# Layer 0 of a four-layer network: two forms of the votes in one tile, a share in a single bank, and a reciprocal moved off VectorE

## The chip, the core and the metric

The kernel runs on one core of a Trainium2 chip. Its engines are TensorE (matrix products, written to PSUM), VectorE, ScalarE, GpSimd (which does not touch PSUM here) and SyncE, whose queue issues most DMAs. The metric is device microseconds of one execution. The profile's short names are PE, PEld (TensorE's weight loads), DVE (VectorE), ACT (ScalarE), POOL (GpSimd) and SP (SyncE).

## The reference, cut to what matters

The input x is 8 images of 16 channels of 256 x 256, fp32. Four layers follow, each as x = x + layer(groupnorm(x)). The change is in layer 0 alone, a convolution whose result is routed between the eight images (axis a):

```
def squash(t, axis=0):
    norm = jnp.linalg.norm(t, axis=axis)
    n2 = norm * norm
    return n2 * t / ((1.0 + n2) * norm)
votes = conv(tensor, w)                  # 3x3, 16 -> 8*16 channels, reshaped n, atoms, cout, h, w
logits = zeros
for _ in range(3):
    r = softmax(logits, axis=0)
    preds = einsum('abcde,abde->bcde', votes, r)
    preds = squash(preds, axis=0)
    logits = logits + einsum('abcde,bcde->abde', votes, preds)
```

In the reference's letters the softmax runs over axis a, the images, the sum with weights r also over a, and the norm of the squash over b, the atoms; this is done three times for every pixel.

## The kernel before, in words

Before layer 0 the statistics of the first norm are taken (`stats0`, to about 95 us), and layers 1 to 3 come after it; none of that is changed. Layer 0 works on 64 tiles of four image rows. For each tile:

- `prepare` (L464) loads x for the tile two further on (`xs`, L470), normalizes it with one product per half (`pd`, L479) and a ScalarE move (L482) and writes it, padded, to a DRAM tensor `d0` (L491), so that rows of all channels and images lie side by side.
- The tile has two halves h of two rows each. For each h, two DMAs (L513) load `kt[h]`: 128 partitions, which are two column shifts times four padded rows times 16 channels, of all eight images. `votes` (L524) makes, for each row j and each half g of the images, one group: two whole products (128 rows of contraction, L533) for column taps 0 and 1, and two products of 64 rows (L537) for column tap 2. The four padded rows serve both j with weights that are zero where a row does not belong. ScalarE copies the group to `v[h]` (L542).
- `squash` (L561) takes a norm: two squares on ScalarE (L569), products that add over the atoms into `n2` (L573), a root by Ln and Exp on ScalarE (L587 to L589), a numerator, a denominator and a reciprocal on VectorE (L593 to L595), and one product on GpSimd (L599): the factors f, 128 x 128. This is done three times per tile.
- `factor` (L606) spreads f over the atoms by products (`fb`, L617). `logits` (L628) multiplies the prediction by it (L635), then all votes by that (`pr`, L643), and sums over c with products (`pl`, L653). In the first routing step the result goes to `ls` by a ScalarE copy (L686); in the second it is copied (L675) and added on GpSimd (L680).
- `softmax` (L691) transposes (`lg`, L700), subtracts the greatest (L706, L707), takes exp on ScalarE (L712), divides (L716 to L718), transposes back (`rt`, L724) and copies to `rs` (L733).
- `weighted` (L736) spreads `rs` by 32-row products (`rb`, L751), in terms of images (4, 5), (6), and (0, 1), (2, 3); VectorE makes `dd` from it and the votes (L762), and GpSimd adds all (L771) to `s`.
- At the end the prediction is scaled (L813), GpSimd adds x (`res`, L816), ScalarE takes statistics (L828), and SP stores the result (L839, L840, L846, L848).

Buffers are counted. `xs` and `res` share the one place of kind `io`. `kt` has two places, `v` six (three tiles in flight), `f` two, `dd` four. In PSUM, kind `x` has three places of two banks (pd, cv, fb and rb take them) and `u` two of one bank (n2, pl, lg, rt).

The order of the work is not that of the code. Each step is recorded as an operation of one engine with what it reads and writes (`_Order.op`, L226). `_Order.run` (L252) then issues, of all operations that are ready and whose buffers are free, the one with the least due time. The due time is the tile's number times a period plus an entry of the list `TIMES`, one for each operation of a tile (L256), so the list decides which tiles' work stands next to which on each engine. Engines then run their own instructions in that order and wait for each other by semaphores.

Of the kernel before, what the change touches and what calls it, by code (L numbers as in the profile page):

```python
# [10 lines left out]
F32 = mybir.dt.float32  # L11
AF = mybir.ActivationFunctionType
ALU = mybir.AluOpType
# [5 lines left out]
P = 128  # L19
WP = W + 2  # L20
# [10 lines left out]
def _consts():  # L31

    p = np.arange(P)
    hi, lo = p // 16, p % 16

    fold = np.stack([h * 16 + lo[:, None] == np.arange(32)[None, :] for h in range(2)], 1)
    unfold = np.zeros((4, 2, C, 2, 4, P), np.float32)
    for h in range(2):
        for k in range(4):
            unfold[k, h, :, h, k] = 0.5 * (np.arange(C)[:, None] == lo[None, :])  # L40


    sel = np.stack([16 * g + 8 * h + hi[:, None] == np.arange(32)[None, :] for g in range(2) for h in range(2)], 1)
    spread = np.zeros((4, 2, 2, 8, 2, 2, 8, C), np.float32)
    for g in range(2):
        for h in range(2):
            for b in range(8):
                spread[:, g, h, b, g, h, b] = 1.0

    diff = np.zeros((B, C, C, B), np.float32)  # L50
    for i in range(C):
        for a in range(B - 1):
            diff[a, i, i, a] = 1.0
            diff[B - 1, i, i, a] = -1.0
        diff[:, i, i, B - 1] = 1.0 / B
    parts = {

        "pair": 0.5 * (p[:, None] // 2 == p[None, :] // 2),
        "diff": diff.reshape(P, P),

        "fold": fold.reshape(P, 2 * 32),
        "unfold": unfold.reshape(P, 8 * P),

        "sel": sel.reshape(P, 4 * 32),

        "spread": spread.reshape(P, 4 * P),
        "ident": np.eye(P),

        "group": (lo[:, None] // 2 == lo[None, :] // 2) / 16.0,

        "same_lo": lo[:, None] == lo[None, :],
        "ones": np.ones((P, P)),
        "mean": np.full((P, P), 1.0 / P),

        "same_c4": lo[:, None] == p[None, :] % 64 // 4,

        "hi8": hi[:, None] == np.arange(8)[None, :],
        "row0": p[:, None] == np.arange(16)[None, :],

        "middle": -(p[:, None] % 4 - 1.5),  # L80

        "pad": _padding(),


        "keep": np.stack([p >= 16, (p < 48) | (p >= 64), p >= 64, p < 64], 1),

        "ident3": _ident3(),
    }
    at = 0
    cols = []  # L90
    for name, a in parts.items():
        a = np.asarray(a, np.float32)
        _CONST[name] = (at, a.shape[1])
        at += a.shape[1]
        cols.append(a)
    return np.ascontiguousarray(np.concatenate(cols, 1))
# [39 lines left out]
def _layout(w0, bw, sw, sc, bias, wq, bq, wk, bk, wv, bv, w3):  # L136
# [1 line left out]


    w0 = w0.reshape(3, 3, C, P)  # L140
    l0 = np.zeros((2, 2, 4, C, 2, P), np.float32)
    for j in range(2):
        for kh in range(3):
            for dx in range(2):
                l0[0, dx, j + kh, :, j] = w0[kh, dx]
                l0[1, dx, j + kh, :, j] = w0[kh, 2]
    l0 = l0.reshape(2, P, 2 * P).transpose(1, 0, 2)


    sw = sw.transpose(1, 4, 2, 3, 0).reshape(C, 2, 4, 81 * C).transpose(0, 2, 1, 3).reshape(64, 2 * 81 * C)  # L150
# [28 lines left out]
class _Buf:  # L179
# [10 lines left out]


TIMES = [
    -723.29, -126.96, -1287.20, -291.27, -719.97, -693.08, -625.75, -683.80, -169.92, -158.78, -153.36,
    -1032.45, -146.30, -286.26, -145.45, -1375.99, -151.90, -338.16, -261.20, -230.76, -136.99, -214.63,
    -126.67, -136.17, -143.63, -139.13, -140.10, -174.81, -899.84, -137.38, -135.05, -211.64, -133.88, -127.93,
    -109.08, -115.69, -139.61, -115.29, -118.15, -149.20, -107.32, -110.73, -165.19, -382.13, -97.75, -92.86,
    -92.25, -91.12, -89.08, -198.43, -88.34, -238.75, -240.66, -85.79, -84.47, -254.75, -133.10, -336.72,
    -223.36, -77.68, -126.26, -82.81, -264.25, -217.14, -78.43, -75.92, -107.53, -72.84, -47.31, -266.51,
    -185.51, -154.67, -555.69, -72.72, -216.04, -93.74, -182.88, -41.32, -30.68, -276.56, -149.62, -123.61,
    -28.12, -118.42, -27.48, -29.71, -88.26, -84.70, -24.63, -62.07, -138.31, -998.81, -338.10, -23.75, -71.35,  # L200
    -168.85, -21.77, -17.87, -1189.68, -15.52, -17.81, -78.48, -11.77, 13.13, -11.07, 16.57, -105.36, -162.33,
    31.16, -216.22, 15.81, 16.90, 16.88, -188.95, 24.25, 29.14, 26.46, 33.82, -255.28, -124.68, -124.23,
    -285.23, -135.30, -169.10, -92.14, -167.00, 36.88, -40.85, -558.24, -220.65, -113.85, -402.73, -159.96,
    35.14, -89.25, 53.60, 71.24, -670.06
]


# [79 lines left out]
class _Net:  # L287
# [123 lines left out]
    def layer0(self, wd, bd, less0, tiles=range(TILES)):  # L411
# [8 lines left out]
        with ExitStack() as st:  # L420
# [1 line left out]
            self.constants(one, "fold", "ident")  # L422
            sbuf = st.enter_context(tc.tile_pool(name="l0_sb", bufs=2))
            psum = st.enter_context(tc.tile_pool(name="l0_ps", bufs=1, space=PSUM))
            w = one.tile([P, 2, 2, P], F32, name="w0")
            nc.sync.dma_start(out=w.rearrange("p s j m -> p (s j m)"), in_=self.d["l0"].rearrange("p s f -> p (s f)"))
            tiny = one.tile([P, 1], F32, name="tiny")
            nc.vector.memset(tiny, 1e-18)
            stats = self.const.tile([P, 2, 2 * TILES], F32, name="st1")
            ident = self.k["ident"]  # L430
            fold = self.k["fold"].rearrange("p (h m) -> p h m", h=2)
            unfold = self.k["unfold"].rearrange("p (h k m) -> p h k m", h=2, k=4)
            sel = self.k["sel"].rearrange("p (g h m) -> p g h m", g=2, h=2)
            spread = self.k["spread"].rearrange("p (g h m) -> p g h m", g=2, h=2)
            ROW = P * WP
# [16 lines left out]
                )  # L452
            nc.sync.dma_start(out=self.d0[(H + 2) * ROW :].unsqueeze(0), in_=ring[0][0:1, 0, 0:16])

            places = dict(io=1, kt=2, v=6, sq=2, f=2, ls=3, e=2, rs=2, s=3, pr=2, dd=4)
            banks = dict(x=3, u=2)
            order = _Order({**places, **banks}, 61.05, TIMES)

            def buf(kind, shape, name=None):
                pool = psum if kind in banks else sbuf  # L460
# [36 lines left out]
            def work(i):  # L497
# [3 lines left out]
                def op(*a, **k):  # L501
                    ops.append(order.op(*a, **k))
# [1 line left out]
                if i + 2 < TILES:  # L504
                    prepare(i + 2, op)

                kt = [buf("kt", [P, 8 * WP]) for _ in range(2)]
                for h in range(2):
                    for dx in range(2):

                        def fetch(h=h, dx=dx):
                            at = (4 * i + 2 * h) * ROW + dx
                            nc.sync.dma_start(  # L513
                                out=kt[h]()[dx * 64 : dx * 64 + 64],
                                in_=self.d0[at : at + 4 * ROW].rearrange("(p f) -> p f", f=8 * WP),
                            )

                        op("SP", 0.5, fetch, [("d0", i), ("d0", i + 2 * h - 1)], [(kt[h], dx)], lag=6.0)
                res = buf("io", [P, 2, 512], "res")


                v = [buf("v", [P, 8, 512]) for _ in range(2)]

                def votes(h, j, g):  # L524


                    ps = buf("x", [P, 2, 512], "cv")

                    def products():
                        t = kt[h]().rearrange("p (a w) -> p a w", a=8)  # L530
                        for n in range(2):
                            a = 4 * g + 2 * n
                            nc.tensor.matmul(ps()[:, n], w[:, 0, j, :], t[:, a : a + 2, 0:W], start=True, stop=False)  # L533
                        for n in range(2):
                            a = 4 * g + 2 * n
                            at = slice(n * 64, n * 64 + 64)
                            nc.tensor.matmul(  # L537
                                ps()[:, n], w[at, 1, j, :], t[at, a : a + 2, 2 - n : 2 - n + W], start=False, stop=True
                            )

                    def move():
# [2 lines left out]
                            ps().rearrange("p n (a w) -> p (n a) w", w=W),  # L544
                        )

                    op("PE", 3.2, products, [(kt[h], 0), (kt[h], 1)], [(ps, 0), (v[h], "turn")], mode="votes")
                    op("ACT", 1.1, move, [(ps, 0)], [(v[h], g, j)])

                def voted(h, a):  # L550
                    return [(v[h], a // 4, 0), (v[h], a // 4, 1)]

                for g in (1, 0):
                    for h in range(2):
                        for j in range(2):
                            votes(h, j, g)

                def rows(ap):
                    return ap.rearrange("p (r w) -> p r w", w=W)
# [1 line left out]
                def squash(s, read):  # L561
# [29 lines left out]
                    def divide():  # L591
                        t, u, den, q = (f()[:, n] for n in range(4))
                        nc.vector.scalar_tensor_tensor(den, n2(), 1.0, t, ALU.add, ALU.mult)  # L593
                        nc.vector.tensor_tensor(u, u, n2(), ALU.add)
                        nc.vector.reciprocal(den, den)  # L595

                    def times():
                        t, u, den, q = (f()[:, n] for n in range(4))
                        nc.gpsimd.tensor_tensor(q, u, den, ALU.mult)  # L599

                    op("ACT", 1.1, root, [(n2, 0)], [(f, 2)])
                    op("DVE", 1.3, divide, [(n2, 0), (f, 2)], [(f, 4)])
                    op("POOL", 0.4, times, [(f, 4)], [(f, 3)])
                    return f

                def factor(f, h, also=()):  # L606
# [4 lines left out]
                    def products():  # L611
                        for b in also:
                            b()
                        for n in range(2):
                            for j in range(2):
                                at = slice(64 * j, 64 * j + 64)
                                nc.tensor.matmul(  # L617
                                    fb()[:, j, n * P : n * P + P],
                                    unfold[at, h, 2 * j + n, :],
                                    f()[at, 3],  # L620
                                    start=True,
                                    stop=True,
# [113 lines left out]
                def weighted(rs):  # L736
# [3 lines left out]
                    for h in range(2):  # L740

                        def term(images, h=h):

                            rb = [buf("x", [P, 2, 512], "rb") for _ in images]

                            def products():
                                for pair, r in zip(images, rb):
# [982 lines left out]
```

## Time and profile before

| | us |
|---|---|
| median of the runs shown (three) | 6453.93 |
| lowest and highest | 6452.06, 6459.32 |
| the profiled execution | 6451.19 |
| its span | 6448.7 |
| layer 0, steady part | from about 200 to about 3330 |

The profiled execution's granted clock was 0.989. In the page, each digit of the slices is the busy share of a fortieth of the span (161 us) in tenths. A group's row names line, engine, operation, written and read tiles, shapes and count, then busy time and the mean of one, and last the idle time before it on its engine with what ended it. A TensorE product of fp32 shows as two instructions, so "x4" is two products. Busy times of matmuls overlap, so blocks are better read in the timeline, from the start of one to the start of the next. The chain of waits follows the work that ended last back through whatever released each step.

### The profile page before, as it was taken

Reading aid. Unit: us, or ns where it says so; the run is one execution under the profiler, and the core shown is the slowest. Engines: PE = TensorE matmul, PEld = TensorE weight load, DVE = VectorE, ACT = ScalarE, POOL = GpSimd, SP = SyncE. Lnnn points to the kernel's source line nnn. Section 1 sums busy time; section 2 is a strip of 40 time slices with the busy share of each in tenths; the row PEclk is TensorE's granted clock in tenths of the full one; section 3 lists DMA queues with packets and bytes.
Section 4 is the critical chain, followed back from the end, with each engine's and each line's share of the span. In section 5 each row is a group of like instructions: output and inputs, shape, how many; then the busy total and the mean of one; then the engine's idle time right before and its main releaser. Section 6 shows DMA issues by size and latency. Waiting matters only on the chain.

```text
span 6448.7 us, 109346 instructions
## 1 busy us (share of the span) xinstructions
PE 6078.3 (94%) x44488; PEld 2716.0 (42%) x44488; DVE 5060.9 (78%) x5963; ACT 2967.9 (46%) x4474; POOL 3394.3 (53%) x2464
## 2 busy tenths in 40 slices
PE   2999999999999999999995999999999999999998
PEld 1333333333333333333332444444444566666653
DVE  5788888888888888888886999999999633333331
ACT  0344444444444444444433888888888422112221
POOL 0577777777777777777775434334433211111123
PEclk9999999999999999999996999999999999999999
DMA  7333333333333333333323555555556543434358
GB/s 270 77 94 99 98 98 92 92 98 93 100 96 100 92 92 98 92 101 94 100 69 95 184 180 173 175 178 174 176 180 179 158 82 90 89 83 93 90 176 267
DMA packets 379593, 800.62 MB, mean 124 GB/s; under 512 B 57426, under 2 KB 191154, under 8 KB 343890
## 3 DMA queue, kind: packets, MB, share of 16 engines
q1 hardware_dynamic: 335250, 730.35, 40.4%
q0 software_dynamic: 9856, 29.20, 1.6%
q10 hardware_dynamic: 33984, 34.08, 1.5%
q8 instruction: 349, 5.72, 0.4%
q14 instruction: 154, 1.26, 0.1%
HBM read 582.77 MB, written 210.77 MB: 123 GB/s over the span
## 4 chain that ended last, share of the span: by engine, by line
PE 58%; DVE 32%; issue 4%; DMA 3%; ACT 1%; POOL 1%; SPq 0%; DVEq 0%; POOLq 0%; ACTq 0%
PE cv L533 13%; PE cv L537 7%; PE pqk L1455 7%; DVE bases L1009 7%; PE pl L653 6%; PE rb L751 5%; DVE e L999 4%; DVE pr L643 4%; PE po L1482 4%; DVE dd L762 4%; PE psc L1470 3%; PE pv L1462 3%; PE p L1547 3%; DVE a L999 2%; DVE a L978 2%
## 5 line engine op out<-in xcount | busy, mean ns | idle before, releaser
L771 POOL TENSOR_TENSOR dd<-dd 128x1024 f32<-128x1024 f32 x512 | 1209.0, 2361 | 338.7 <-DVE dd L762 318.4
L1032 PE MATMUL ps<-bases,tw 128*32 128x512 f32 (+1 forms) x13824 | 1361.7, 545 | 16.7 <-POOL bases L1001 6.7
L762 DVE SCALAR_TENSOR_TENSOR dd<-rb,v 128x1024 f32<-128x1024 f32 (+1 forms) x1024 | 1078.0, 1084 | 214.3 <-PE rb L751 175.5
L1001 POOL TENSOR_TENSOR bases<-e,a 128x1024 f32<-128x1024 f32 (+1 forms) x264 | 621.7, 2378 | 928.1 <-DVE e L999 927.8
L542 ACT COPY v<-cv 128x1024 f32<-128x1024 f32 x512 | 518.7, 1013 | 1281.2 <-PE cv L537 1281.2
L643 DVE TENSOR_TENSOR pr<-v,fb 128x2048 f32<-128x2048 f32 (+1 forms) x512 | 1010.9, 2015 | 32.0 <-PE pl L653 28.1
L533 PE MATMUL cv<-kt,w 128*128 128x512 f32 x2048 | 1009.1, 615 | 11.2 <-DMA kt<-d 9.4
L1032 PEld LDWEIGHTS ps<-bases,tw 128*32 128x32 f32 x13824 | 598.2, 109 | 801.7 <-issue 482.9
L771 POOL TENSOR_TENSOR s<-s,dd 128x512 f32<-128x512 f32 x512 | 653.3, 1276 | 30.1
L751 PE MATMUL rb<-rs,ct_fold 32*128 32x512 f32 x3584 | 605.6, 649 | 9.1 <-ACT rs L733 2.4
L533 PEld LDWEIGHTS cv<-kt,w 128*128 128x128 f32 x2048 | 347.0, 189 | 558.8 <-issue 392.7
L537 PE MATMUL cv<-kt,w 64*128 64x512 f32 x2048 | 578.8, 641 | 0.0
L653 PE MATMUL pl<-pr,ct_fold 128*32 128x512 f32 x3584 | 531.6, 605 | 45.4 <-DVE pr L643 45.2
L1466 ACT ACTIVATE vt<-pv,w_b2v 128x128 f32<-128x128 f32 x512 | 146.5, 368 | 840.2 <-PE pv L1462 840.2
L771 POOL TENSOR_TENSOR s<-v,dd 128x512 f32<-128x512 f32 x256 | 325.9, 1273 | 340.0 <-DVE dd L762 330.9
L1455 PE MATMUL pqk<-w_qk,t 128*128 128x512 f32 x1024 | 482.9, 594 | 4.7 <-POOL t L1449 4.6
L1487 DVE TENSOR_TENSOR y<-po,res 128x512 f32<-128x512 f32 x128 | 88.5, 691 | 493.9 <-PE po L1482 468.5
L1009 DVE SCALAR_TENSOR_TENSOR bases<-xr,xm,bases 128x1024 f32<-128x1024 f32 (+1 forms) x264 | 447.9, 1734 | 0.3 <-POOL bases L1001 0.3
L1449 POOL TENSOR_TENSOR t<-t,emb 128x512 f32<-128x512 f32 x128 | 162.5, 1270 | 514.0 <-DVE t L1445 494.3
L986 ACT ACTIVATE sq<-a 128x1024 f32<-128x1024 f32 (+1 forms) x264 | 263.7, 999 | 231.4 <-DVE a L978 230.7
L968 ACT ACTIVATE d<-xr,bd,sd 128x1024 f32<-128x1024 f32 (+1 forms) x264 | 319.0, 1208 | 14.1 <-DMA xr<-x1p 14.1
L751 PEld LDWEIGHTS rb<-rs,ct_fold 32*128 32x128 f32 x3584 | 173.0, 185 | 351.0 <-issue 118.2
(269 smaller groups left out, 8430.3 us busy)
## 6 DMA issues: line engine op xcount, KB each, us to landing
kt<-d SPq DMA_DIRECT2D x256, 516.0 KB
xr<-x1p SPq DMA_DIRECT2D x120, 1024.0 KB
d<-dn ACTq DMA_DIRECT2D x64, 516.0 KB
x<-y SPq DMA_DIRECT2D x128, 258.0 KB
xs<-in_x_dram SPq DMA_DIRECT2D x16, 2048.0 KB
xs<-in_x_dram SPq DMA_DIRECT2D x64, 512.0 KB
res<-in_x_dram SPq DMA_DIRECT2D x64, 512.0 KB
x<-s SPq DMA_DIRECT2D x128, 256.0 KB
```

Source lines behind the costliest of these rows:

```text
L533: nc.tensor.matmul(ps()[:, n], w[:, 0, j, :], t[:, a : a + 2, 0:W], start=True, stop=False)
L537: nc.tensor.matmul(ps()[:, n], w[at, 1, j, :], t[at, a : a + 2, 2 - n : 2 - n + W], start=False, stop=True)
L542: nc.scalar.copy(v[h]()[:, 4 * g : 4 * g + 4, j * W : j * W + W], ps().rearrange("p n (a w) -> p (n a) w", w=W),)
L643: nc.vector.tensor_tensor(pr()[:, :n].rearrange("p n (r w) -> p n r w", w=W), v[h]()[:, 4 * g : 4 * g + n].rearrange("p n (r w) -> p n r w ...
L653: nc.tensor.matmul(pl()[at : at + 32], sel[:, g, h, :], pr()[:, t, :], start=h == 0 and g == 0, stop=h == 1 and (g == 1 or t == 3),)
L751: nc.tensor.matmul(r()[:, n], spread[at, g, h, :], rs()[at], start=True, stop=True)
L762: nc.vector.scalar_tensor_tensor(dd()[:, :n], r()[:, :n], 1.0 / B, v[h]()[:, a : a + n], ALU.subtract, ALU.mult)
L771: op("POOL", us, lambda: nc.gpsimd.tensor_tensor(out[0](), a[0](), b[0](), ALU.add), a[1] + b[1], out[1])
L1001: nc.gpsimd.tensor_tensor(ring[n % 3][:, 0, p : p + m, 1 : 1 + W], rows(e), rows(a), ALU.subtract)
L1009: nc.vector.scalar_tensor_tensor(r, rows(part[1]), xm[:, b : b + 1], v, ALU.is_gt, ALU.mult)
L1032: nc.tensor.matmul(out if k is None else out[:, k], lhs, rhs, start=start, stop=stop, skip_group_check=True)
L1455: nc.tensor.matmul(ps, t[:, n, k * P : (k + 1) * P], wqk[:, n, :], start=n == 0, stop=n == 1)
```

## The change

Four things are changed, all in layer 0.

1. Votes in two forms. For h = 1 nothing but names changes (`wide`, `votes_wide`). For h = 0 each row j gets loads of its own: `kt` holds eight of the nine taps times 16 channels in 128 partitions (two DMAs), and `kr` holds the ninth, in four groups of 32 partitions, one for each pair of images (one DMA; the upper 16 partitions of a group have the tap's weights, the others zeros). Then `rest` makes four products of 32 rows into two `x` buffers, and `most` adds two whole products to each. The weights `l0` now hold both forms, 768 columns in place of 512.
2. The lone share of a term, image 6, takes a one-bank buffer of kind `u` (`r6`) instead of a two-bank one of kind `x`.
3. The reciprocal in the squash: instead of VectorE's, ScalarE takes Ln and Exp with scale -1, and GpSimd does one Newton step, four operations instead of one.
4. `TIMES` is a new list, with an entry for each operation of the new tile, and the period in the due times is 48 instead of 61.05.

The constant `unfold` also becomes half as wide, since both pairs of its blocks were alike.

```
-            order = _Order({**places, **banks}, 61.05, TIMES)
+            places = dict(io=1, kt=2, kr=2, v=6, sq=2, f=2, ls=3, e=2, rs=2, s=3, pr=2, dd=4)
+            order = _Order({**places, **banks}, 48, TIMES)
...
+                def votes(h, j):
+                    kt = buf("kt", [P, 8 * WP])
+                    kr = buf("kr", [P, 2 * WP])
+                    at = (4 * i + 2 * h + j) * ROW
...
+                    def fetch():
+                        rows_at(kt()[:96], 0, [[1, 2], [8 * WP, 48], [1, 8 * WP]])
+                    def fetch2():
+                        rows_at(kt()[96:], 2, [[8 * WP, 32], [1, 8 * WP]])
+                    def fetch3():
+                        rows_at(kr(), 16 * 8 * WP + 2, [[2 * WP, 4], [8 * WP, 32], [1, 2 * WP]])
...
+                    ps = [buf("x", [P, 2, 512], "cv") for _ in range(2)]
+                    def most(g):
+                        t = kt().rearrange("p (a w) -> p a w", a=8)
+                        for n in range(2):
+                            a = 4 * g + 2 * n
+                            nc.tensor.matmul(ps[g]()[:, n], w[:, 0], t[:, a : a + 2, 0:W], start=False, stop=True)
+                    def rest():
+                        for g in range(2):
+                            for n in range(2):
+                                at = slice(64 * g + 32 * n, 64 * g + 32 * n + 32)
+                                t = kr()[at].rearrange("p (a w) -> p a w", a=2)[:, :, 0:W]
+                                nc.tensor.matmul(ps[g]()[:, n], w[at, 1], t, start=True, stop=False)
+                    op("PE", 1.1, rest, [(kr, 0)], [(p, 0) for p in ps] + [(v[h], "turn")], mode="last")
...
-                for g in (1, 0):
-                    for h in range(2):
+                for h in range(2):
+                    if h in (0,):
                         for j in range(2):
-                            votes(h, j, g)
+                            votes(h, j)
+                    else:
+                        wide(h)
...
-                        nc.vector.reciprocal(den, den)
+                    def inverse():
+                        t, den = f()[:, 0], f()[:, 2]
+                        nc.scalar.activation(t, den, AF.Ln)
+                        nc.scalar.activation(t, t, AF.Exp, scale=-1.0)
                     def times():
-                        t, u, den, q = (f()[:, n] for n in range(4))
-                        nc.gpsimd.tensor_tensor(q, u, den, ALU.mult)
+                        r, u, den, q = (f()[:, n] for n in range(4))
+                        nc.gpsimd.tensor_tensor(den, den, r, ALU.mult)
+                        nc.gpsimd.tensor_tensor(q, u, r, ALU.mult)
+                        nc.gpsimd.tensor_scalar(den, den, -1.0, 2.0, ALU.mult, ALU.add)
+                        nc.gpsimd.tensor_tensor(q, q, den, ALU.mult)
...
-                            rb = [buf("x", [P, 2, 512], "rb") for _ in images]
+                            rb = [buf("x", [P, 2, 512], "rb") if len(a) == 2 else buf("u", [P, 1, 512], "r6") for a in images]
```

## The prediction

> **What bounds the kernel now.** First the page's busy row and slices, then a table of windows, to see where layer 0 lies and which engine fills it:
>
> ```profile
> PE 6078.3 (94%) x44488; PEld 2716.0 (42%) x44488; DVE 5060.9 (78%) x5963; ACT 2967.9 (46%) x4474; POOL 3394.3 (53%) x2464
> ...
> PE   2999999999999999999995999999999999999998
> ...
> POOL 0577777777777777777775434334433211111123
> ```
>
> ```profile
> 1200.00:1600.00 400.00, 383.19 (x2264) 144.95 (x2266) 358.64 (x381) 170.86 (x298) 306.05 (x203) 1.00 0.37 97
> 1600.00:2000.00 400.00, 383.20 (x2284) 144.99 (x2280) 357.42 (x384) 169.38 (x298) 303.33 (x204) 1.00 0.37 97
> ```
>
> The columns are TensorE, its weight loads, VectorE, ScalarE, GpSimd, the granted clock, the DMA share and GB/s. Layer 0 is steady from about 200 to 3330 us, at full clock. One tile of four rows takes 51.36 us: in the chain of the window 800 to 2800 the same VectorE piece stands at 838.85 and, 38 tiles on, at 2790.37. Of these 51.36, TensorE is busy 49.2, VectorE 46.0, GpSimd 38.9, ScalarE 21.8.
>
> Next the groups of the window 800 to 2800, forms kept apart (busy, mean ns):
>
> ```profile
> L533 PE MATMUL cv<-kt,w 128*128 128x512 f32 x1248 | 613.8, 614 | 0.4
> L751 PE MATMUL rb<-rs,ct_fold 32*128 32x512 f32 x2180 | 359.7, 640 | 4.0
> L537 PE MATMUL cv<-kt,w 64*128 64x512 f32 x1248 | 352.2, 641 | 0.0
> L595 DVE RECIPROCAL f<-f 128x128 f32<-128x128 f32 x117 | 110.4, 944 | 0.0
> L599 POOL TENSOR_TENSOR f<-f 128x128 f32<-128x128 f32 x116 | 53.1, 457 | 9.8 <-DVE f L595 9.8
> ```
>
> Mean matmul times hold the pipeline, so I price blocks by the timeline of one tile, from start to next start:
>
> ```profile
> 1658.81 1.14 PE L751 MATMUL rb<-rs,ct_fold 32*128 32x512 f32 x8
> 1659.88 1.99 PE L533 MATMUL cv<-kt,w 128*128 128x512 f32 x4
> 1661.80 1.13 PE L537 MATMUL cv<-kt,w 64*128 64x512 f32 x4
> 1662.86 1.14 PE L751 MATMUL rb<-rs,ct_fold 32*128 32x512 f32 x6
> 1664.73 0.66 PE L724 MATMUL rt<-ct_fold,e 128*128 128x128 f32 x4 [0.74 <-DVE e L718]
> ```
>
> A block of four 32-row products (eight instructions) takes 1.07, two whole products (x4) 1.92, the 64-row block 1.06 (0.96 ahead of fb). A vote group is 2.88 to 2.98, on average 2.95. A tile holds eight vote groups (23.6), eight rb blocks (8.55), four sevens of pl (7.7), six fb (3.25), three n2 (1.65), two lg and two rt (2.25) and pd (1.85): 48.85. The other 2.5 are waits: 0.74 for the softmax above, about 0.55 each at pd (VectorE's dd) and pl (VectorE's pr), the rest in small ones.
>
> Last, the chain between 1100 and 1220. In some tiles it leaves TensorE and runs through the load of x:
>
> ```profile
> 1145.48 2.51 POOL s L816 x2
> ...
> 1150.28 1.32 SPq L846
> 1151.64 7.80 DMA xs<-in_x_dram
> 1159.58 1.96 PE pd L479 x4
> ```
>
> xs and res share one buffer, so xs can be asked for only after GpSimd's last add, and in the queue it stands behind five stores. Alone, at the start (chain at 104.76), the load took 3.65. So TensorE bounds layer 0, with VectorE 5.4 us behind.
>
> **Votes, h = 0 only.** Removed per tile: four vote groups, 4 x 2.95 = 11.8. Added, for each of two j: one block of four 32-row products (L751's row, 1.07) and four whole products (2 x 1.92 = 3.84), together 2 x 4.91 = 9.82. TensorE falls by 1.98 to 46.87. The 32-row block is the same form as L751, on four row groups and four banks; bounds are 1.07 and, did the four not overlap, 3.84 as for whole products. I take 1.07, since rows and shape are those of the row. The rows hold the change of row grouping: 1.06 instead of 0.96 where the next block has another grouping.
>
> By the Trainium skill, "TensorEngine Tiling (Array Packing)", Key Properties, changing the tiling mode drains TensorE, which speaks against mixed forms. Read by the rows that drain is about 0.1 per change and the new form has no more changes, so the sum would be unmoved; were a drain worth a whole 32-row block, four of them would undo the gain. No row here shows such a drain.
>
> Moves to v stay at eight ScalarE copies of 1.01. What moves is the loads: h = 0 now loads two kt and two kr, 2.6 MB instead of 1.03, so a tile moves about 6.5 MB instead of 4.9 (96 GB/s x 51.36), and the DMA share goes from 0.37 to about 0.5. SP issues eight loads for four. Two kt places serve three loads: the wide load can start only when the first kt of the tile has been read, and it is used after rb, rb, pl, fb, lg, the next 32-row block, four whole products and rt: 1.07 + 1.07 + 1.92 + 0.54 + 0.54 + 1.07 + 3.84 + 0.59 = 10.6. The first kt load (chain at 113.27) took 8.32, so it is hidden. If it took 12, it would cost 1.4 a tile, 90 us.
>
> **Reciprocal.** VectorE loses 3 x 0.944 = 2.83 a tile: 43.1. ScalarE gains six operations like L588 (0.31): 23.7 with ample idle time. GpSimd gains nine small ones: 9 x 0.457 = 4.1, so 43.0. Its tensor_scalar is in no row; bounds are the 128x2 copy (0.19) and the 128x512 add (1.27); I take L599's 0.457, the same size. None of this is TensorE's time; what counts is whether f is late for fb. The chain from n2 was root 1.05, VectorE 1.34, GpSimd 0.46 and four hops of 0.1: 3.25. Now it is 1.05 + 0.45 + 0.65 + 1.83 and five hops: 4.5. TensorE's work between n2 and fb was 4.9, 5.3 and 11.2; in the new order it is 7.9 (four whole products, two rb, pl), 6.5 (half a pl, fb, a vote group, rb, half a pl) and 7.0 (pl, fb, rb, lg, a vote group). The cover left is 3.4, 2.0 and 2.5, for queueing; before it was 1.65, 2.05 and 7.9. Where it is gone, each microsecond of lateness is one of TensorE's, 64 us over the tiles. Behind the new wait on ScalarE stand the pl copy and the softmax's exp; behind that on GpSimd the next dd adds.
>
> By the Trainium skill, "GPSIMD Engine Reference", 4.1 Engine selection, elementwise work belongs on VectorE, since GpSimd takes about twice as long for two inputs. The trace agrees: 457 ns (L599) against 276 (L594) for the same tile. By engine time alone the edit is a loss of about 1.05 us a squash, 200 us in all if it lay on the path; by the idle 12 us that GpSimd has in each tile it is nothing.
>
> **Single-bank share.** The lone rb product goes to pool u (r6), so a term takes one two-bank buffer of three instead of two. In the new order each r6 follows a u buffer that was read before. Between no gain and the 0.5 at pd, I count it within the waits below.
>
> **Order.** I laid one period of the new order out by these durations. Four waits of TensorE remain: the second half of a 32-row block and the fb after it, whose x buffers VectorE's dd frees late (0.4 + 0.3); rb behind a vote copy (0.1); lg right behind pl with only fb (0.54) beside ScalarE's copy, 0.6 plus hops (0.3); the other lg, behind GpSimd's ls add, which stands after a 2.36 and two 1.27 adds (0.8). Sum 1.9, against 2.5 before; period 46.87 + 1.9 = 48.8. The load of xs now stands ahead of the stores: some 6.4 us of cover against 3.65 alone, so that loop no longer ends last (7.80 would cost 1.4).
>
> **Sum.** 64 x (51.36 - 48.8) = 164 us. Filling is the same chain of loads; draining, the last tile's three squashes have no cover, 3 x 1.25 = 4. The profiled execution took 6451.2 (span 6448.7): 6451.2 - 164 + 4 = 6291. The median of the runs shown is 2.7 above it: **6294 us**.
>
> **Rivals.**
> 1. The gain is half given back: f or ls on GpSimd, now 43 of 49 us busy and in order, comes late behind 2.36 us adds. For: two of the three covers are under 2.6, little over one add. Against: three tiles are in flight. Waits of 3.2 give 50.1 and 6453.9 - 81 + 4 = 6377.
> 2. Slower: the same queue, but each f starts a 2.36 and a 1.27 add later than laid out. Then 3.63 less the covers is 0.2 + 1.6 + 1.1 = 2.9 more waiting, 4.8 in all, period 51.7: 6453.9 + 22 + 4 = 6480. It decides from 4.5 us of waits a tile. For it: GpSimd shows waits of up to 4.9 us for dd, so its work is bunched. Against: before, f waited 9.8 us in 39 tiles. TensorE would pay more if a wait passed some 3 us: after 4.0 idle at 3390.43 pl x8 took 1.93 instead of 1.06.
> 3. Nothing comes of it: the loop through xs, or a kt load, still sets 51.3. About 6455. Against: the stores are moved behind xs.
>
> **How the numbers follow.** Forecast 0.69, rival 1 0.17, rival 2 0.10, rival 3 0.04. About 0.2% is what a measurement can tell from no change: faster 0.86, same 0.04, slower 0.10. Low end: half the waits (0.9), 47.8, 6453.9 - 228 + 4 = 6230. High end: waits of 4.0, 50.85, 6453.9 - 33 + 4 = 6425, past rival 1; out are rivals 2 and 3 and a small tail.
>
> **What would show it.** Right: a period near 48.8, vote lines 2 us less per tile, no reciprocal of f on VectorE, GpSimd near 43 of 49, r6 without waits. Wrong: TensorE waiting for f or ls on GpSimd by more than 1 us a time, waiting for kt or xs, a 32-row vote block over 1.2, or GpSimd's small operations over 0.6.

## The result

The changed kernel takes 7036.45 us (median of four, 7024.81 to 7041.18) beside 6455.55 for the kernel before on the same chip: a ratio of 1.0897, 95% interval 1.0878 to 1.0916. The forecast was 6294. The profiled execution took 7024.81, its span is 7023.0.

**The profile after.** The page's busy row, two of its slices, the chain, and the two whole-product vote groups:

```profile
PE 6156.0 (88%) x44488; PEld 2783.7 (40%) x44488; DVE 4918.4 (70%) x5771; ACT 3074.2 (44%) x4858; POOL 3607.6 (51%) x3040
...
PE   1788888888888888888888779999999999999998
...
PEclk8999999999999999999999889999999999999999
...
DMA d<-dn 14%; DMA kt<-d 11%; PE cv L586 8%; PE pqk L1534 6%; DVE bases L1088 6%; PE cv L590 4%; DVE e L1078 4%; PE po L1561 3%; PE psc L1549 3%; PE pv L1541 3%; PE rb L830 3%; PE p L1626 3%; DVE a L1078 2%; DVE a L1057 2%; DVE e L1057 2%
```

```profile
L586 PE MATMUL cv<-kt,w 128*128 128x512 f32 x1024 | 602.2, 718 | 359.5 <-DMA kt<-d 358.2
...
L549 PE MATMUL cv<-kt,w 128*128 128x512 f32 x1024 | 573.1, 712 | 217.7 <-DMA kt<-d 217.7
```

TensorE no longer fills layer 0, and it waits for loads of `kt`: 358 us at the wide votes (L586), 218 at the new ones (L549). No engine's own work heads the chain any more, but two DMAs: the write of `d0` and the load of `kt`. Between 800 and 2800 us a tile takes 59.83 (the residual add's semaphore at 817.4 and, 33 tiles on, at 2791.9) in place of 51.36. The first residual add is at 342.6 in place of 272.2, so the start is 70 us later too: the first load of `kt` stands in the chain with 39.63 us, where it took 8.32 before.

One tile. First TensorE's timeline, then the chain of the same stretch (start, us, what):

```profile
2046.42 1.14 PE L556 MATMUL cv<-kr,w 32*128 32x512 f32 x8
2050.95 5.29 PE L549 MATMUL cv<-kt,w 128*128 128x512 f32 x8 [3.38 <-DMA kt<-d]
2056.07 0.60 PE L803 MATMUL rt<-ct_fold,e 128*128 128x128 f32 x4
2062.72 3.75 PE L586 MATMUL cv<-kt,w 128*128 128x512 f32 x4 [6.05 <-DMA kt<-d]
2066.40 1.83 PE L590 MATMUL cv<-kt,w 64*128 64x512 f32 x4
```

```profile
2032.67 16.42 DMA d<-dn
2049.14 0.57 SPq L528
2050.37 12.22 DMA kt<-d
2062.72 3.75 PE cv L586 x4
```

And the DMA engines in the same stretch (last two columns: DMA share, GB/s; the one before is the granted clock):

```profile
2034.00:2036.00 2.00, 2.00 (x18) 0.45 (x11) 2.00 (x2) 1.97 (x6) 2.00 (x3) 1.00 1.01 303
...
2038.00:2040.00 2.00, 2.00 (x6) 0.83 (x5) 2.00 (x4) 1.09 (x3) 1.92 (x2) 1.00 0.13 56
...
2046.00:2048.00 2.00, 1.57 (x12) 0.57 (x11) 1.70 (x3) 0.00 (x0) 1.67 (x2) 1.00 0.13 56
2048.00:2050.00 2.00, 0.00 (x0) 0.00 (x0) 1.27 (x3) 0.58 (x1) 1.92 (x2) 1.00 0.12 50
...
2052.00:2054.00 2.00, 2.00 (x4) 0.94 (x3) 2.00 (x2) 0.00 (x0) 1.78 (x2) 0.50 1.02 187
```

From 2038 to 2050 the share is 0.12 to 0.13, two of sixteen DMA engines, at 50 to 56 GB/s, while TensorE first works and then stands still. The packets in it are the new `kt` load's, 8256 bytes, 0.313 us each, and packets of the `d0` write, 1032 bytes, on the same two engines in turn: 46 of each between 2039 and 2047. The trace's landing events show the same by shares. Of the 16 shares of the `d0` write, 14 have landed by 2037.98, the last two at 2048.65 and 2049.09; the new load, asked for at 2028.51, has two shares in all, at 2049.60 and 2050.02. So the write of `d0` ends after 16.42 us, and SP, which works in order, holds what is behind it:

```profile
SPq L528 <- DMA d<-dn: 581.8, 33, 18.6
```

That is 17.6 us a tile at the head of SP's queue (a `kr` load), with the wide `kt` load (L609) behind it. When that load is issued, its 12.22 us are half in the open (TensorE waits 6.05). After each wait TensorE runs at half clock for some us (0.50 in the window from 2052): L549's block takes 5.29, L586's 3.75, L590's 1.83.

### The profile page after: what moved, and what is told of

The parts are those of the page before. It is cut to its first block, busy times and chain, and to the rows that moved or that the text cites. A ratio compares the mean times of both kernels' runs of the same rounds, so it can differ in the third digit from the quotient of the medians.

```text
span 7023.0 us, 110704 instructions
## 1 busy us (share of the span) xinstructions
PE 6156.0 (88%) x44488; PEld 2783.7 (40%) x44488; DVE 4918.4 (70%) x5771; ACT 3074.2 (44%) x4858; POOL 3607.6 (51%) x3040
## 2 busy tenths in 40 slices
DMA packets 404947, 902.04 MB, mean 128 GB/s; under 512 B 58194, under 2 KB 191922, under 8 KB 361042
## 4 chain that ended last, share of the span: by engine, by line
PE 40%; DMA 28%; DVE 20%; issue 5%; POOL 4%; ACT 2%; SPq 1%; DVEq 0%; POOLq 0%; ACTq 0%
DMA d<-dn 14%; DMA kt<-d 11%; PE cv L586 8%; PE pqk L1534 6%; DVE bases L1088 6%; PE cv L590 4%; DVE e L1078 4%; PE po L1561 3%; PE psc L1549 3%; PE pv L1541 3%; PE rb L830 3%; PE p L1626 3%; DVE a L1078 2%; DVE a L1057 2%; DVE e L1057 2%
## 5 line engine op out<-in xcount | busy, mean ns | idle before, releaser
L841 DVE SCALAR_TENSOR_TENSOR dd<-rb,v 128x1024 f32<-128x1024 f32 x768 | 907.9, 1217 | 27.9 <-PE r L830 12.8
L586 PE MATMUL cv<-kt,w 128*128 128x512 f32 x1024 | 602.2, 718 | 359.5 <-DMA kt<-d 358.2
L549 PE MATMUL cv<-kt,w 128*128 128x512 f32 x1024 | 573.1, 712 | 217.7 <-DMA kt<-d 217.7
L841 DVE SCALAR_TENSOR_TENSOR dd<-r,v 128x512 f32<-128x512 f32 x256 | 176.3, 689 | 829.5 <-PE r L830 821.0
L732 PE MATMUL pl<-pr,ct_fold 128*32 128x512 f32 x3584 | 505.3, 601 | 4.8 <-DVE pr L722 4.7
L549 PEld LDWEIGHTS cv<-kt,w 128*128 128x128 f32 x1024 | 220.1, 226 | 529.5 <-issue 307.0
L586 PEld LDWEIGHTS cv<-kt,w 128*128 128x128 f32 x1024 | 201.9, 219 | 546.0 <-issue 528.0
```

What stands on the lines that cost most here:

```text
L549: nc.tensor.matmul(ps[g]()[:, n], w[:, 0], t[:, a : a + 2, 0:W], start=False, stop=True)
L586: nc.tensor.matmul(ps()[:, n], w2[:, 0, j, :], t[:, a : a + 2, 0:W], start=True, stop=False)
L732: nc.tensor.matmul(pl()[at : at + 32], sel[:, g, h, :], pr()[:, t, :], start=h == 0 and g == 0, stop=h == 1 and (g == 1 or t == 3),)
L841: nc.vector.scalar_tensor_tensor(dd()[:, :n], r()[:, :n], 1.0 / B, v[h]()[:, a : a + n], ALU.subtract, ALU.mult)
```

## The experiments

**Theory A.** The new load of 96 partitions takes the two column shifts as its outermost dimension, `[[1, 2], [8 * WP, 48], [1, 8 * WP]]`. A load with an outermost count of 2 runs on 2 of the 16 DMA engines: 96 x 8256 bytes at 54 GB/s are some 15 us, and the `d0` write, which has shares on those two engines, ends late with it. **Theory B**: the number of bytes is too much (2.6 MB of `kt` and `kr` for 1.03), however the loads are cut. **Theory C**: the new order of SP's queue holds the wide load back, whatever the first load takes. **Theory D**: the reciprocal's longer chain, or the vote form, slows the kernel by itself. (The expectations number the first three in the same way.)

**1. The same load as two.**

```
-  rows_at(kt()[:96], 0, [[1, 2], [8 * WP, 48], [1, 8 * WP]])
+  for dx in range(2):
+      rows_at(kt()[48 * dx : 48 * dx + 48], dx, [[8 * WP, 48], [1, 8 * WP]])
```

> The changed kernel, but the 96-partition load of kt is made as two loads of 48 partitions, one for each column shift; bytes, buffers and order stay. Theory A (the load whose outermost dimension counts 2 runs on 2 of the 16 DMA engines: 8256-byte packets of 0.313 us, 12 to 13 in 2 us, 54 GB/s, for 14 us, and the write of d0 ends behind it): the load spreads, the write of d0 lands in under 8 us, TensorE no longer waits for kt, a tile takes 48.5 to 49.5 us, the whole 6280 to 6350. Theory B (the 1.6 MB more per tile is too much for the loads, however they are cut): over 6900, as the changed kernel's 7036. Theory C (the new order of SP's queue holds the wide load back, whatever the first load takes): over 6800.

Measured: 6306.23, ratio 0.9771 (0.9756 to 0.9785), inside theory A's range.

**2. The same single load, with the rows outermost** (the weight rows are put in the new order of partitions):

```
-  rows_at(kt()[:96], 0, [[1, 2], [8 * WP, 48], [1, 8 * WP]])
+  rows_at(kt()[:96], 0, [[8 * WP, 48], [1, 2], [1, 8 * WP]])
```

> The changed kernel with the same single load of 96 partitions and the same bytes, but its dimensions swapped: 48 rows outermost, the two shifts inside (the weights' rows are permuted to match). Theory A, if the outermost count decides how a load is spread: within 0.5% of the split kernel, 6280 to 6350. If instead only contiguous runs or the number of loads matters (A wrong in that point): still 7036. Theories B and C: about 7036.

Measured: 6274.02, ratio 0.9726 (0.9711 to 0.9740), 6 us under the expectation and 0.5% below the split load. Bytes, loads and their order in SP's queue are those of the changed kernel, and 762 us are gone. That is theory A; B and C fall, and D cannot be what made the kernel slow, since the reciprocal and the vote form are still there. The pages' packet counts fit as well: under 512 bytes there are 58194 in the changed kernel, 59986 here and 62034 with the split load, so 14 and 30 more for each of the 128 loads, as one small packet for each engine that takes part would give for 16 and twice 16 engines in place of 2. The `kr` load still has an outermost count of 4; no wait for it shows among TensorE's. The waits of TensorE, and the chain of one tile:

```profile
PE cv L587 <- DMA kt<-d: 16.5, 19, 1.9
PE lg L780 <- POOL ls L760: 13.6, 42, 0.3
PE rb L831 <- DVE pr L723: 9.0, 41, 0.2
PE cv L587 <- ACT rs L813: 5.9, 5, 1.2
PE cv L587 <- ACT v L572: 1.4, 2, 0.7
```

```profile
2041.34 7.72 DMA d<-dn
...
2050.35 10.21 DMA kt<-d
```

The `d0` write takes 7.72 for 16.42. The waits sum to 46.4 in 42 tiles, 1.1 a tile, and a tile takes 47.99 (825.4 to 2792.9, 41 tiles). The wide load still takes 10.2, the cover that the prediction laid out being 10.6, so it still ends last in 19 tiles, by 0.9 us on average.

**3. The kernel before, with this form alone**: each half's two loads of 64 partitions become one of 128 with the shift outermost. Same bytes, half the loads.

```
-  out=kt[h]()[dx * 64 : dx * 64 + 64],
-  in_=self.d0[at : at + 4 * ROW].rearrange("(p f) -> p f", f=8 * WP),
+  out=kt[h](),
+  in_=bass.AP(tensor=src.tensor, offset=src.offset, ap=[[1, 2], [8 * WP, 64], [1, 8 * WP]]),
```

> The kernel before, with nothing of the change, but the two loads of each kt (64 partitions each) are made as one load of 128 partitions with the two shifts outermost: the suspected cost alone, with the same bytes and one load fewer. Theory A: 1.03 MB on 2 engines at 54 GB/s is 19 us a load, 38 us a tile on the same two engines, the write of d0 ends behind them and TensorE waits for kt: 6700 to 7600, and a rate near 54 GB/s between bursts. Theories B and C: 6455, within 0.5%, since neither bytes nor order change.

Measured: 6892.30, ratio 1.0678 (1.0662 to 1.0694). The form costs 438 us with none of the change around it. The expectation had the size but not the place: what waits is not the product that reads `kt` but `pd`, whose load of x has shares on the same two engines. Of the one asked for at 1653.17, 14 shares have landed by 1657.46 and the last two at 1662.19 and 1662.26. In the window 800 to 2800:

```profile
PE pd L479 <- DMA xs<-in_x_dram: 179.3, 33, 7.4
```

**4. An outermost count of 3**: three shifts of two kernel rows in the 96 partitions, the other two taps in the 32 (weight rows put in that order).

```
-  rows_at(kt()[:96], 0, [[1, 2], [8 * WP, 48], [1, 8 * WP]])
+  rows_at(kt()[:96], 0, [[1, 3], [8 * WP, 32], [1, 8 * WP]])
-  rows_at(kt()[96:], 2, [[8 * WP, 32], [1, 8 * WP]])
+  rows_at(kt()[96:], 32 * 8 * WP, [[8 * WP, 16], [1, 2], [1, 8 * WP]])
```

> The changed kernel with the 96-partition load cut so that its outermost dimension counts 3 (three shifts, 32 rows each) instead of 2; the 32-partition load takes the remaining two taps with 16 outermost; same bytes, number of loads and order. Theory A in numbers: 3 engines at 26 GB/s each is 79 GB/s, the load takes about 9.8 us instead of 14.3, and stretches with 18 to 20 packets of 8256 bytes in 2 us take the place of those with 12 to 13. The tile lies between the 60.5 us of the changed kernel and the 48.7 of the spread load: 50 to 57, the whole 6380 to 6800. If it were only a matter of two against many (a special case of two), it would be about 6274; if the form of the load didn't matter, 7036.

Measured: 6942.19, ratio 1.0760 (1.0739 to 1.0782). The rate comes near the expected one; the time lies far above the expected range:

```profile
2052.00:2054.00 2.00, 2.00 (x19) 0.85 (x16) 1.37 (x2) 1.36 (x4) 2.00 (x2) 1.00 0.70 219
2054.00:2056.00 2.00, 2.00 (x23) 1.05 (x20) 1.72 (x2) 0.99 (x3) 1.92 (x2) 1.00 0.17 68
...
2060.00:2062.00 2.00, 2.00 (x22) 0.41 (x14) 2.00 (x3) 0.00 (x0) 1.92 (x5) 1.00 0.19 76
```

```profile
2049.96 15.17 DMA d<-dn
...
2066.44 10.41 DMA kt<-d
```

The share is 0.17 to 0.19, three of sixteen. By its landing events the load, asked for at 2045.80, now has three shares and ends at 2062.84: 17.0 us after issue, where the one on two engines needed 21.5 (2028.51 to 2050.02). It is not the expected 9.8, since until 2054 its engines also serve spread transfers (170 to 290 GB/s in all): my expectation took the load as alone on its engines, and that was wrong. The load became 4.5 us shorter, but the `d0` write only 1.25 (15.17 for 16.42): its small packets still take turns with the load's large ones, one for one (49 of each between 2055 and 2061), and now on three engines. So TensorE's wait for the new load is all but gone (9.0 us in the window 800 to 2800, 0.3 a tile, for 2.8), while that for the wide load, behind the write in SP's queue, is 8.5 a tile (290.0 in 34) for 5.8. The special case of two falls, and so does the sum by the load's rate alone.

The Trainium skill, "DMA: Bandwidth & Descriptors", section "Why a DMA increments its semaphore by 16 and not by 1", has the rule: the slowest dimension of each side that is not of size one is taken, and the largest number up to 16 that divides both is the number of DMA engines. For 96 partitions against 2, 3 and 48 rows this gives 2, 3 and 16. The runs agree: shares of 0.12 to 0.13 and 0.17 to 0.19 with two and three landing events, and in experiment 2 sixteen landing events and no stretch of several us near 0.12 in the tile shown.

**5. The kernel before, with the reciprocal moved alone** (ScalarE's Ln and Exp, GpSimd's Newton step; the due times of before, the new step taking that of the division):

```
-                        nc.vector.reciprocal(den, den)
+                        nc.scalar.activation(t, den, AF.Ln)
+                        nc.scalar.activation(t, t, AF.Exp, scale=-1.0)
...
-                        nc.gpsimd.tensor_tensor(q, u, den, ALU.mult)
+                        nc.gpsimd.tensor_tensor(den, den, r, ALU.mult)
+                        nc.gpsimd.tensor_tensor(q, u, r, ALU.mult)
+                        nc.gpsimd.tensor_scalar(den, den, -1.0, 2.0, ALU.mult, ALU.add)
+                        nc.gpsimd.tensor_tensor(q, q, den, ALU.mult)
```

> The kernel before with only the reciprocal moved: Ln and Exp on ScalarE and four GpSimd operations, placed where the reciprocal stood (the due times of the old list, each new step with that of the step it follows). By the prediction's chain of 4.5 us against covers of 4.9, 5.3 and 11.2, two fb wait a little and VectorE has 2.8 us less: 0 to 0.5 us a tile, 6430 to 6490. If the longer chain were what slows the changed kernel by 9 us a tile, half of that at least should show here: over 6700.

Measured: 6804.31, ratio 1.0545 (1.0527 to 1.0562): 350 us, far off what I expected, and over the 6700 that I had named as the sign of theory D. In before's order the longer chain is slow by itself; that it isn't in the new order is shown by experiment 7, and by the changed kernel's own waits, which have none for f. TensorE's longest wait here, and a squash in which it shows:

```profile
PE fb L614 <- POOL f L595: 146.3, 69, 3.4
```

```profile
1691.66 0.65 PE L562 MATMUL n<-sq,ct_fold 128*32 128x128 f32 x16
...
1694.96 0.28 DVE L583 TENSOR_TENSOR f<-f,n 128x128 f32<-128x128 f32 x1
...
1697.25 1.01 ACT L531 COPY v<-cv 128x1024 f32<-128x1024 f32 x1 [2.38 <-PE cv L526]
1698.16 0.31 ACT L587 ACTIVATE f<-f 128x128 f32<-128x128 f32 x1
...
1700.10 0.45 POOL L595 TENSOR_TENSOR f<-f 128x128 f32<-128x128 f32 x1
1700.61 1.22 PE L614 MATMUL fb<-f,ct_fold 64*128 64x128 f32 x8 [3.41 <-POOL f L595]
```

VectorE's part (denominator, then numerator) is done at 1695.24, but ScalarE takes the Ln at 1698.16: in its queue a vote copy stands ahead, which waits for products that TensorE has yet to make. From n2 to f it takes 8.9 us, where before's order leaves 4.9 of TensorE's work between.

**6. The same, with division, inverse and product given the root's due time**, so that the copy can't stand ahead.

```
-  -899.84, -137.38, -135.05,              (root, divide, times in the list of before)
+  -899.84, -899.84, -899.84, -899.84,     (root, divide, inverse, times; so in all three squashes)
```

> As the run with only the reciprocal moved (6804), but the due times of VectorE's divide, ScalarE's inverse and GpSimd's steps are set to that of the root before them, so that ScalarE issues the inverse ahead of the copies of pl and of the votes. Theory: of the 5.5 us a tile most came from the inverse standing behind a vote copy that waits for TensorE (2.4 us idle ahead of it) and so f is 3.4 us late; then 6480 to 6650. If the four GpSimd steps alone make f late: still over 6720.

Measured: 8162.47, ratio 1.2647 (1.2628 to 1.2666). The cure that I drew from experiment 5 is far worse: f still makes fb wait (330.7 us in 76 waits of the window, 4.4 each). The waits of the other engines are longer too (in 1200 to 2800 GpSimd's next step waits up to 7.5 us for the inverse). That the copy ahead of the Ln is the whole cost of experiment 5 is not shown, nor what exactly costs so much here. What the runs show is that the cost of the longer chain depends on the order it stands in.

**7. The reciprocal back on VectorE, in the kernel of experiment 2.**

```
+                        nc.vector.reciprocal(den, den)
...
-                        nc.scalar.activation(t, den, AF.Ln)
-                        nc.scalar.activation(t, t, AF.Exp, scale=-1.0)
+                        return
...
-                        nc.gpsimd.tensor_tensor(den, den, r, ALU.mult)
-                        nc.gpsimd.tensor_tensor(q, u, r, ALU.mult)
-                        nc.gpsimd.tensor_scalar(den, den, -1.0, 2.0, ALU.mult, ALU.add)
-                        nc.gpsimd.tensor_tensor(q, q, den, ALU.mult)
+                        nc.gpsimd.tensor_tensor(q, u, den, ALU.mult)
```

> The rows_first kernel (6274) with the reciprocal back on VectorE and one product on GpSimd, in the new order. By the prediction's sum TensorE bounds the tile and VectorE has slack, so little is lost: VectorE at 46.0 of 48.7 us, 0 to 1 us a tile, 6270 to 6340. If VectorE's 2.8 us are what makes the new period possible: 6400 or more. If the longer squash chain costs TensorE time: under 6260.

Measured: 6321.96, ratio 0.9800 (0.9784 to 0.9817). In the new order the move is worth 48 us, 0.75 a tile, inside the expected range. Theory D falls for the reciprocal. The timeline of one tile shows a place: VectorE's reciprocal (0.94 from 2025.24) stands ahead of the next `pr`, so `dd` reads the first share only at 2028.24, and the four products that follow take 1.80 from start to the next block (2027.64 to 2029.44). In experiment 2 they take 1.07 (1331.31 to 1332.38).

**8. Both halves in the old vote form, in the kernel of experiment 2** (due times mapped, entry for entry).

```
-                    if h in (0,):
+                    if h in ():
```

> The rows_first kernel with the votes of h = 0 in the old form too (eight wide vote groups a tile), the due times of the narrow steps given to the wide ones; the loads fall back to 2.1 MB a tile. By the prediction's blocks TensorE has 1.98 us more a tile: 127 us, 6400, or up to 6480 if three vote groups in a row make it wait. If TensorE doesn't bound the tile: 6274, within 20 us.

Measured: 6451.02 (ten runs), ratio 0.9994 (0.9985 to 1.0004). In this order, which was laid out for it, the vote form is worth 177 us, 2.8 a tile: theory D falls here too. Reciprocal, share and order without the form come out at the time of before.

**9. The lone share in two banks again, in the kernel of experiment 2.**

```
-  rb = [buf("x", [P, 2, 512], "rb") if len(a) == 2 else buf("u", [P, 1, 512], "r6") for a in images]
+  rb = [buf("x", [P, 2, 512], "rb") for a in images]
```

> The kernel with the shifts innermost, but the lone share of image 6 takes a two-bank buffer of kind x again, as before the change; the due times stay, so a term holds two x places of three while it runs. The prediction counted this edit as between nothing and 0.5 us a tile, within the other waits. If the waits at x places are short (pd, cv and rb together wait under 1 us a tile in the kernel with the shifts innermost), one more x place in use is worth up to that: 6274 to 6310 us. The other theory, that the place is what lets the new order run at all, since its 32-row vote block takes two x places at once beside the terms: each term then holds back the next block until VectorE has read it, 1 to 2 us a tile, 6340 to 6400 us.

Measured: 6620.67, ratio 1.0255 (1.0241 to 1.0269). 347 us, 5.4 a tile, more than either theory, in the direction of the second. Two terms in a row, seven products (three and then four), in this kernel, and then in that of experiment 2:

```profile
1306.96 2.31 PE L831 MATMUL rb<-rs,ct_fold 32*128 32x512 f32 x10
1309.49 1.13 PE L831 MATMUL rb<-rs,ct_fold 32*128 32x512 f32 x4 [0.22 <-DVE dd L842]
1310.54 1.92 PE L733 MATMUL pl<-pr,ct_fold 128*32 128x512 f32 x14
```

```profile
1330.14 0.70 PE L831 MATMUL rb<-rs,ct_fold 32*128 32x512 f32 x2
...
1331.31 1.14 PE L831 MATMUL rb<-rs,ct_fold 32*128 32x512 f32 x8
1332.38 1.92 PE L733 MATMUL pl<-pr,ct_fold 128*32 128x512 f32 x14
```

3.58 us from start to the next block, against 2.24. Seven products with four two-bank buffers need one place more than the three there are, so TensorE waits in the middle until VectorE has read one. A tile has four such pairs of terms, though one pair does not stand in a row. From 1294.81 on, the tile of this kernel has them 1.96, 1.34, 1.25 and 1.18 longer than that of experiment 2 (the last by its three products alone): 5.7, all of what the tile shown is longer (52.91 for 47.26), and near the 5.4 on average. The planner may also put steps elsewhere for want of a place, so that the order was not held fixed here.

## Why the prediction was wrong

- **The step that failed** is the loads: "The first kt load (chain at 113.27) took 8.32, so it is hidden. If it took 12, it would cost 1.4 a tile, 90 us." These sentences price the wide load alone, by the row of a load of its own form (64 partitions, rows outermost). The new load, with two shifts outermost, got no time of its own: I counted its bytes and the share, 0.5, of all sixteen engines, and the rest was put at nothing. It had two engines, and needed 21.5 us in a tile; the first one stands in the chain with 39.63. For the wide load the price was low but inside the cover once the new load is spread: 10.2 for 8.32, against 10.6.
- That TensorE would wait for `kt` was among the signs of being wrong, but what followed was in no rival with its price: the `d0` write ends behind the slow load, SP holds the wide load behind the write, and TensorE waits 8.6 a tile ((198.8 + 93.9) / 34, the window's waits for `kt` at L586 and L549; experiment 2 has 0.4). Half clock after the waits adds 1.6 at L549, 1.8 at L586 and 0.7 at L590 in the tile shown: 8.2 + 4.1 = 12.3, against 59.83 - 47.99 = 11.8 on average (the tile shown waits 9.4, more than the average). Rival 3 had the place ("a kt load"), but at 51.3 as the least period, not 59.8; rival 2, the slower one, had the wrong mechanism: GpSimd's `ls` makes `lg` wait 0.3 a tile here, and f none that the list shows.
- **Half clock** was named, after waits of some 3 us. The window from 2052 to 2054 shows 0.50 after a wait of 3.38. The Trainium skill, "TensorE: Matmul & The Clock Gate", section "What's actually happening", says that the clock halves after an idle window of about 3.4 us; the trace agrees.
- **Votes**: with the load spread, TensorE's period less its waits is 47.99 - 1.1 = 46.9, the 46.87 of the prediction. The 32-row block took 1.07 to 1.15, taken at 1.07; the block of four whole products 3.54 to 3.63, taken at 3.84. So the form takes 9.4 a tile in place of 9.82, and four wide groups in experiment 8 take the 11.8 of the prediction: 2.4 of the 2.8. The rest goes with waits: without the form `fb` waits 0.8 a tile for f (31.8 in 39), with it the wide votes wait 0.4 for `kt`. (The eight vote groups of the timeline before come to 23.3, not 23.6, the shortest being 2.77 and not 2.88; the sum of the blocks is that much smaller and the waits before that much larger.)
- **Reciprocal**: the tensor_scalar takes 300 ns beside the 456 to 459 of its neighbours, which the prediction took it to equal (and 457 against VectorE's 276 is 1.7 times, a little under the "about twice" that it says the trace agrees with):

```profile
L676 POOL TENSOR_SCALAR f<-f 128x128 f32<-128x128 f32 x100 | 30.0, 300 | 0.0
```

  "None of this is TensorE's time" held in the new order, where the covers were laid out at 6.5 to 7.9. In before's order the same move costs 350 us, though the prediction's chain of 4.5 fits the covers of 4.9 and 5.3 there: in the squash shown it took 8.9, most of the rest being queueing, for which the prediction had left room but no number. That the move gives 48 us in the new order had no term: VectorE, 5.4 us behind TensorE by busy time, still stood in its way at one place of the tile.
- **Single-bank share**: "Between no gain and the 0.5 at pd" was too low by a factor of ten. In this order, which sets up to seven products side by side, the place carries 5.4 a tile.
- **Order**: waits of 1.9 were laid out, 1.1 are there with the load spread; the GpSimd `ls` wait is 0.3, not 0.8. The start was not the same "chain of loads": even in experiment 2 the first residual add is 23 us later than before (295.2, 272.2). With 63 tiles at 51.04 - 47.90 = 3.14 less (first to last residual add), 23 - 198 = -175 is the difference of the spans.

With that one dimension swapped the kernel takes 6274, against the 6294 on record: near, but in part by errors that cancel. The waits came out 0.8 a tile better than laid out, the start 23 us worse, and the reciprocal and the single bank carry what no term had.

## What to carry to other kernels

Price a load by its access pattern, not by its bytes alone: the outermost count decided how many DMA engines it got (two, three and sixteen here), and a row of the profile answers only for loads of the same form. A slow load also delayed each transfer that shared its engines, and with it whatever stood behind that transfer in an issuing queue. A longer chain or one buffer less is judged in its order: the same move of a reciprocal cost 350 us in the one order and gave 48 in the other.

## What the runs showed of the hardware

- In the stretches shown two engines carry 50 to 56 GB/s, three 68 to 76, in packets of 8256 bytes that take 0.313 us. A third engine made the load 4.5 us shorter (17.0 for 21.5).
- Where two transfers met on an engine, their packets took turns one for one, whatever their size: 46 of 8256 bytes and 46 of 1032. The write of the small ones, 516 KB, took 16.42 us so, and 7.72 beside a spread load.
- A small tensor_scalar of GpSimd on 128 x 128 takes 300 ns, a tensor_tensor of the same size 450 to 460.
